# The last mixing steps of a graph layer: operands moved from SBUF to PSUM, and a list of steps scheduled anew

## The chip, the cores and the metric

The kernel runs on one core of one Trainium2 chip. The metric is the device time of one execution in microseconds; where several runs are shown, their median. Five engines work side by side, each through its own queue in order: TensorE (PE; its weight loads are PEld), VectorE (DVE), ScalarE (ACT), GpSimd (POOL) and SyncE (SP), which here only issues transfers. TensorE writes its results to the eight banks of PSUM; the other memory on the core is SBUF. [...]

## The reference

Four graph layers follow one another over x (8 batches, 2048 nodes, 64 features) and one adjacency matrix (2048 x 2048); each is `x = layernorm(x + layer(x, adj))`. The change lies in the end of layer 1, whose last lines and normalization are:

```
pair = jnp.stack([industry, g], axis=2)
coefs2 = jax.nn.softmax(attn_scores(pair), axis=-1)
out = jnp.einsum('bnk,bnkf->bnf', coefs2, pair)
...
def attn_scores(f):
    return jnp.tanh(f @ fcW + fcb) @ av
...
x = _layernorm(x + out, axis=-1)
```

`industry` is the adjacency applied to a projection of x, and `g` comes from attention over hyperedges. A softmax over two is a sigmoid of the difference of the two scores, and the kernel computes it so: with s = tanh(difference / 2), the mix is g + 0.5 (1 + s) (industry - g).

## The kernel before, in words

A tile is 128 nodes by 512 values (8 batches of 64 features), and there are 16 tiles. Layer 0 and the preparation of layer 1 take the first 660 us. Layer 1 then works on 16 tiles in a software pipeline: each tile has some forty small steps, and several tiles are under way at once. The order is written out by hand, as one long string of tokens at the end of `layer1` (L1183 to L1258): `3.m0` is step m0 of tile 3. `perform` calls the steps in this order, and `program_order` (L213) makes the queues of TensorE, VectorE, ScalarE and GpSimd keep it; SyncE's transfers may go ahead of it, as far as free buffers allow. Since each queue is in order, an instruction that waits holds everything behind it on its engine.

The steps of one tile j:

- `i` (L656), eight times: four matmuls of 128 x 512 each (L1918) into the bank `ind`, the adjacency product; `ind` (L668) is ScalarE's copy of it to SBUF. `mask` and `xr` and the start of `sx` are transfers from HBM.
- `sx`, `ST`, `gates`, `tau` (L866 to L905): small gate values. `gp`, `dp`, `red` are matmuls (L936, L954, L985), `m`, `z`, `e`, `g` VectorE's steps on 1024 or 512 values (L944, L947, L966, L988), `exp` and `t3` ScalarE's (L950, L960), `ch`, `w`, `a0`, `ga` GpSimd's (L925, L971, L978, L981). Together they make `g`, one SBUF row of 512 values.
- The mixer (L1001 to L1116): `dlt` (L1008) is industry - g; `xg` (L1018) is g + x on GpSimd, in the row `r`; `tr`, `sT`, `fc`, `th`, `sub` turn both inputs, multiply them with fcW and take the tanh; `df` (L693, in `by_columns`) multiplies by av and leaves the score differences in one PSUM bank; `rw` (L1055) is the tanh of the difference, `rt` (L168) turns it with two transposes into the other half of the same bank, so that each node has its eight shares there, in eight separate columns (`column_view`).
- Then the steps of the change: `sw` (L1065), ScalarE copies the eight shares to SBUF; `mult` (L1071), VectorE makes dlt = (share + 1) dlt; `r` (L1076), r = 0.5 dlt + r; `s` (L1082), the sum over 64 features; `centre` (L1086), r = r - s / 64. All of them read and write SBUF rows, apart from the copy's source.
- `sq`, `var`, `rstd`, `x2` (L1092 to L1106): squares on ScalarE, their sum on VectorE, the inverse root on GpSimd, eight scaled copies on ScalarE.

Layer 2's first steps stand in the tail of the same list: `f` (transposes), `xT`, `mm` (L1146), `hi`, `add`, `lo` (L1152 to L1160), and `A`, the first adjacency products.

PSUM is divided among pools in this part: one bank for the adjacency product, two for gathers (`g`), two single-bank buffers with the tag "m", which `dp`, `red`, the two turned rows and layer 2's `f` take in turns, one bank "sm" that `sx` and `df` take in turns, and two for `fc`. A step that needs a buffer waits until the last reader of what was in it is done. In the list before, 80 steps take an "m" buffer. The score bank "sm" is free again when ScalarE's copy `sw` has read it.

Of the kernel before, what the change touches and what calls it, by code (L numbers as in the profile page):

```python
# [9 lines left out]
F32 = mybir.dt.float32  # L10
# [3 lines left out]
ALU = mybir.AluOpType  # L14
# [49 lines left out]
def kernel(  # L64
# [547 lines left out]
    def layer1(  # L612
# [76 lines left out]
        def by_columns(dst, th):  # L689
            for half in range(2):  # L690
                for h in range(2):
                    k = 2 * half + h
                    nc.tensor.matmul(  # L693
                        dst[32 * k:32 * k + 32, 0:2 * P], av32,
                        th[:, h, half * 2 * P:(half + 1) * 2 * P],
                        start=True, stop=True, tile_position=(0, 32 * k),
                    )

        def column_view(src):
            return src[:, 2 * P:4 * P].rearrange(  # L700
                "p (l f h e) -> p l f h e", l=2, f=2, h=2
            )[:, :, :, :, 0]
# [6 lines left out]
        with tc.tile_pool(name="fa", bufs=2) as fa:  # L709
# [10 lines left out]
            with program_order():  # L720
# [69 lines left out]
                def capped():  # L790
                    c["ese"] = fa.tile([P, B], F32, tag="ese", name="ese", bufs=1)
                    nc.vector.tensor_scalar(
                        c["ese"].rearrange("p (f l h) -> p l f h", l=2, h=2),
                        column_view(c["sp"]), TOP, None, op0=ALU.min,
                    )
# [206 lines left out]
        def mixer(j):  # L1002
# [60 lines left out]
            def shares():  # L1063
                t["sw"] = small("sw", f"sw_{j}")
                nc.scalar.copy(  # L1065
                    t["sw"].rearrange("p (f l h) -> p l f h", l=2, h=2), column_view(t["df"])
                )

            def shared():
                dlt = b_view(t["dlt"])  # L1070
                nc.vector.scalar_tensor_tensor(  # L1071
                    dlt, bcast(t["sw"]), 1.0, dlt, op0=ALU.add, op1=ALU.mult
                )

            def mixed():
                nc.vector.scalar_tensor_tensor(  # L1076
                    t["r"], t["dlt"], 0.5, t["r"], op0=ALU.mult, op1=ALU.add
                )

            def summed():  # L1080
                t["s"] = small("s", f"s_{j}")
                nc.vector.tensor_reduce(t["s"], b_view(t["r"]), AX.X, ALU.add)  # L1082

            def centred():
                r = b_view(t["r"])
                nc.vector.scalar_tensor_tensor(  # L1086
                    r, bcast(t["s"]), -1.0 / C, r, op0=ALU.mult, op1=ALU.add
# [10 lines left out]
            def deviation():  # L1098
                nc.gpsimd.tensor_scalar(t["var"], t["var"], EPS, None, op0=ALU.add)
                t["rstd"] = small("rstd", f"rstd_{j}")  # L1100
                nc.gpsimd.tensor_tensor(t["rstd"], t["var"], mhalf, ALU.pow)

            def normed():
# [8 lines left out]
                rw=rows, rt=rows_turned, sw=shares, mult=shared, r=mixed, s=summed, centre=centred,  # L1112
# [67 lines left out]
        with program_order():  # L1180
            perform(
                (
                    "0.xr 1.xr c.rests 0.sx 0.dp 0.ST 0.gates 0.gp0 0.tau 1.sx 0.ch0 0.m0 0.gp1 1.ST "  # L1183
                    "1.dp 1.gates 0.m1 0.ch1 1.tau 2.sx 0.z0 1.i 1.ch0 0.t3 2.gates 1.i 0.exp0 0.z1 "
                    "1.i 2.tau 0.e0 0.exp1 1.gp0 1.ch1 2.ST 0.e1 1.ind 2.i 0.w0 1.t3 1.m0 1.gp1 2.i "
                    "1.z0 0.w1 2.i 0.a0 1.exp0 2.i 1.m1 0.ga 1.e0 0.red 3.sx 1.z1 2.ch0 2.gp0 3.ST "
                    "2.dp 0.g 1.exp1 2.m0 1.w0 0.tr0 2.i 0.sT0 1.e1 0.tr1 2.i 2.z0 0.xg 2.xr 0.sT1 "
                    "0.fc0 0.dlt 2.exp0 1.a0 3.gates 2.i 0.th0 1.w1 2.e0 2.i 3.tau 0.fc1 2.ind 2.ch1 "
                    "2.gp1 0.th1 3.i 2.m1 2.w0 2.t3 0.sub 1.red 4.sx 1.ga 2.z1 3.dp 4.ST 4.gates 2.a0 "
                    "3.i 2.exp1 1.g 0.df 4.tau 3.ch0 2.e1 1.tr0 0.rw 3.i 1.sT0 1.dlt 0.rt 3.gp0 2.w1 "  # L1190
                    "0.sw 0.mult 1.fc0 3.m0 1.tr1 1.th0 3.i 1.xg 3.xr 0.r 1.sT1 3.z0 3.i 2.ga 1.fc1 "
                    "0.s 3.exp0 3.ch1 0.centre 3.i 1.th1 3.e0 2.red 3.t3 1.sub 4.ch0 5.sx 3.gp1 2.g "
                    "5.ST 3.i 0.sq 3.m1 3.w0 2.dlt 2.tr0 3.i 5.mask 3.z1 2.sT0 2.fc0 3.ind 2.xg 4.xr "
                    "5.gates 3.exp1 4.i 0.var 3.a0 5.tau 1.df 3.e1 2.tr1 1.rw 0.rstd 4.i 2.th0 4.gp0 "
                    "2.sT1 1.rt 4.dp 4.m0 1.sw 3.w1 0.x2 4.i 1.mult 4.z0 2.fc1 4.ch1 4.i 1.r 4.exp0 "
                    "3.ga 1.s 3.red 2.th1 4.e0 6.sx 4.t3 3.g 4.i 5.ch0 1.centre 4.gp1 2.sub 6.ST 4.i "
                    "1.sq 3.xg 5.xr 4.m1 3.tr0 3.tr1 1.var 3.sT0 4.i 4.w0 3.sT1 4.z1 3.fc0 6.gates "
                    "4.exp1 5.dp 1.rstd 3.dlt 6.tau 4.e1 2.df 4.i 6.mask 3.th0 4.a0 5.gp0 4.ind 3.fc1 "
                    "5.m0 4.w1 2.rw 1.x2 2.rt 5.i 5.z0 5.i 5.ch1 2.sw 5.exp0 2.mult 4.red 4.ga 2.r "
                    "5.t3 7.sx 5.e0 5.i 4.g 7.ST 6.ch0 3.th1 5.gp1 2.s 4.tr0 5.m1 4.tr1 4.sT0 5.i "  # L1200
                    "4.dlt 5.w0 4.sT1 5.z1 6.dp 3.sub 5.exp1 5.i 4.xg 6.xr 2.centre 4.fc0 5.e1 5.a0 "
                    "2.sq 5.i 2.var 5.w1 6.gp0 7.gates 5.i 6.m0 7.tau 3.df 6.ch1 5.i 7.mask 3.rw 6.z0 "
                    "4.th0 3.rt 5.ga 5.red 5.ind 4.fc1 6.exp0 2.rstd 5.g 5.dlt 6.i 3.sw 6.t3 6.e0 "
                    "5.tr0 6.i 3.mult 5.sT0 7.ch0 6.gp1 4.th1 3.r 8.sx 6.m1 2.x2 6.i 3.s 6.w0 6.z1 "
                    "5.tr1 6.i 8.ST 4.sub 5.sT1 5.xg 7.xr 7.dp 6.exp1 3.centre 5.fc0 6.a0 6.e1 3.sq "
                    "6.i 3.var 6.w1 7.gp0 8.gates 6.i 7.m0 8.tau 4.df 3.rstd 6.i 4.rw 7.z0 5.th0 4.rt "
                    "6.i 8.mask 7.exp0 6.ga 6.red 6.ind 7.e0 7.ch1 5.fc1 4.sw 3.x2 4.mult 8.ch0 9.sx "
                    "6.g 7.gp1 9.gates 7.t3 7.i 6.xg 8.xr 7.m1 6.tr0 6.dlt 7.i 6.sT0 7.z1 7.w0 9.ST "
                    "5.th1 6.tr1 8.dp 4.r 7.exp1 5.sub 7.i 7.a0 9.tau 7.e1 6.sT1 5.df 6.fc0 5.rw 4.s "
                    "7.w1 8.gp0 4.centre 6.th0 5.rt 7.i 8.m0 5.sw 4.sq 8.ch1 6.fc1 5.mult 8.z0 7.ga "  # L1210
                    "7.i 8.t3 7.red 4.var 8.exp0 5.r 4.rstd 7.i 7.g 6.th1 10.sx 8.e0 7.i 10.ST 4.x2 "
                    "6.sub 9.ch0 7.tr0 7.i 9.mask 5.s 10.gates 8.gp1 7.sT0 8.w0 9.dp 7.ind 8.m1 "
                    "5.centre 10.tau 6.df 8.z1 5.sq 8.i 7.xg 9.xr 6.rw 7.fc0 7.dlt 8.exp1 8.a0 5.var "
                    "8.i 7.th0 8.e1 5.rstd 7.tr1 8.i 7.sT1 9.gp0 8.w1 8.i 5.x2 9.m0 6.rt 8.i 9.z0 "
                    "6.sw 9.ch1 7.fc1 6.mult 9.exp0 8.ga 8.i 6.r 9.t3 8.red 9.e0 8.i 8.g 10.ch0 7.th1 "
                    "6.s 9.gp1 8.tr0 9.m1 8.i 10.mask 8.sT0 6.centre 9.w0 10.dp 9.z1 8.ind 6.sq 9.i "
                    "7.sub 9.exp1 8.xg 10.xr 11.sx 6.var 8.fc0 9.a0 9.e1 11.ST 8.tr1 11.gates 6.rstd "
                    "9.i 8.sT1 8.dlt 11.tau 7.df 10.gp0 8.th0 9.w1 9.i 10.m0 7.rw 8.fc1 6.x2 10.z0 "
                    "7.rt 10.ch1 9.i 10.exp0 9.ga 9.red 9.i 10.t3 10.e0 9.i 9.g 11.ch0 8.th1 10.gp1 "
                    "9.i 7.sw 10.m1 10.w0 7.mult 12.sx 10.z1 9.i 11.mask 12.ST 9.tr0 7.r 9.ind 9.xg "  # L1220
                    "11.xr 11.dp 12.gates 9.sT0 10.exp1 9.dlt 9.tr1 10.a0 10.i 8.sub 9.sT1 12.tau "
                    "10.i 10.e1 8.df 7.s 10.w1 10.i 8.rw 7.centre 8.rt 9.fc0 7.sq 8.sw 7.var 11.ch1 "
                    "10.i 9.th0 8.mult 7.rstd 11.gp0 8.r 11.t3 10.i 11.m0 10.red 10.ga 7.x2 8.s 10.i "
                    "11.z0 13.sx 10.g 11.exp0 10.i 8.centre 10.xg 12.xr 13.gates 10.tr0 13.ST 8.sq "
                    "10.i 12.mask 11.e0 10.sT0 12.dp 10.ind 8.var 12.ch0 11.gp1 10.dlt 11.i 11.m1 "
                    "10.tr1 13.tau 11.z1 11.w0 11.i 9.fc1 11.exp1 8.rstd 11.i 9.th1 11.e1 11.i 10.sT1 "
                    "9.sub 11.a0 8.x2 12.gp0 11.i 12.m0 11.w1 9.df 10.fc0 12.z0 9.rw 12.ch1 9.rt "
                    "10.th0 11.i 11.ga 11.red 12.exp0 11.i 12.t3 12.e0 10.fc1 11.g 12.w0 9.sw 12.gp1 "
                    "9.mult 10.th1 11.i 13.mask 12.m1 11.tr0 10.sub 11.ind 13.ch0 14.sx 11.sT0 12.i "
                    "12.z1 14.ST 11.fc0 12.a0 11.dlt 12.exp1 14.gates 12.i 11.xg 13.xr 12.e1 14.tau "  # L1230
                    "10.df 12.i 9.r 11.th0 12.w1 9.s 13.gp0 10.rw 12.i 13.m0 10.rt 13.ch1 12.i 10.sw "
# [1433 lines left out]
```

## Time and profile before

| what | value |
|---|---|
| time before, median of 3 runs | 1230.51 us (1228.17 to 1231.52) |
| the profiled execution | 1229.4 us, its span 1227.7 us |
| busy over the span: PE / DVE / ACT / POOL | 97% / 74% / 32% / 42% |
| granted TensorE clock over the span | 0.995 |
| VectorE's busy time in slices 23 to 30 of 40 | about nine tenths |
| DMA | 157.10 MB, mean 128 GB/s |

The profile is one execution, recorded by the hardware. "Busy" is the time with an instruction in work; matmuls are pipelined and their ends are modelled, so a busy TensorE is not a full one. A row of a group names the line, the engine, the operation, output <- inputs, the shapes and the count; then busy us and mean ns of one; then how long the engine idled just before these instructions, and what ended that. A timeline row gives start and duration in us first. A row of waits gives the engine and line that waited, what it waited for, and then us in total, times, and the longest.

### The profile page before, as it was taken

To read this page: it belongs to the slowest core of one execution; us is meant where nothing else is said; L and a number is where in the kernel's file an instruction comes from. 1 tells how busy PE (TensorE), PEld (TensorE's weight loads), DVE (VectorE), ACT (ScalarE), POOL (GpSimd) and SP (SyncE) were. 2 spreads that over 40 slices of the span, in tenths; PEclk is the share of its full clock that TensorE was granted. 3 is DMA by queue.
4 is the path that set the end of the run, shared out by engine and by line. 5 is a ranking of instruction groups with operands and counts; after the bars stand their busy time and mean duration, and the time that the engine had idled before them with its cause. 6 is when DMAs were issued, how large, how long until landed. Compare 5 with 4: busy or idle time off the path is not lost.

```text
span 1227.7 us, 19772 instructions
## 1 busy us (share of the span) xinstructions
PE 1187.7 (97%) x7470; PEld 942.0 (77%) x7470; DVE 911.2 (74%) x1671; ACT 388.8 (32%) x1019; POOL 512.4 (42%) x429
## 2 busy tenths in 40 slices
PE   9999899999999999999999999999999999999996
PEld 7777788888888888888886655555557788888885
DVE  4555678888888888888876899988996766665454
ACT  3100102222222222222223667676676411111111
POOL 2000472555555555555511788888881700000000
PEclk9999999999999999999998999999999999999998
DMA  8977943333333333332384113122320333334541
GB/s 282 251 230 222 189 131 104 109 105 113 109 103 107 114 115 114 106 99 99 106 309 147 43 61 110 62 103 104 95 69 2 138 132 109 118 123 163 180 172 71
DMA packets 101848, 157.10 MB, mean 128 GB/s; under 512 B 13041, under 2 KB 64369, under 8 KB 96113
## 3 DMA queue, kind: packets, MB, share of 16 engines
q1 hardware_dynamic: 96944, 151.38, 38.4%
q10 hardware_dynamic: 4368, 4.33, 1.0%
q8 instruction: 61, 1.00, 0.4%
q0 software_dynamic: 432, 0.05, 0.1%
q14 instruction: 43, 0.34, 0.1%
HBM read 117.97 MB, written 37.76 MB: 127 GB/s over the span
## 4 chain that ended last, share of the span: by engine, by line
PE 73%; DVE 13%; DMA 4%; issue 3%; ACT 3%; POOL 2%; SPq 0%; DVEq 0%; ACTq 0%; POOLq 0%
PE pp L1457 26%; PE a L1918 19%; PE y2p L1414 9%; PE y1p L569 5%; PE ind L1918 3%; DMA xraw<-in_xn 2%; DVE d L947 2%; DVE ez L966 1%; DVE gp L944 1%; PE u L1146 1%; DMA adj<-in_at 1%; PE yp L2017 1%; PE try L168 1%; DVE r L1086 1%; PE hp L1582 1%
## 5 line engine op out<-in xcount | busy, mean ns | idle before, releaser
L1468 DVE SCALAR_TENSOR_TENSOR r<-pp,emb_sb,r 128x256 f32<-128x256 f32 x512 | 247.4, 483 | 78.1 <-PE pp L1457 63.9
L1457 PE MATMUL pp<-w_sb,xT 64*128 64x256 f32 x1024 | 155.4, 380 | 0.6 <-DVE r L1468 0.6
L1457 PE MATMUL pp<-w_sb,y2T 64*128 64x256 f32 x1024 | 153.5, 376 | 2.4 <-DVE y2T L1430 2.4
L1457 PE MATMUL pp<-w_sb,y1T 64*128 64x256 f32 x1024 | 153.3, 376 | 0.0
L1326 POOL TENSOR_TENSOR ms<-msk,srow 128x1024 f32<-128x1024 f32 x30 | 76.5, 2552 | 93.8 <-DVE msk L449 93.8
L1457 PEld LDWEIGHTS pp<-w_sb,y2T 64*128 64x128 f32 x1024 | 99.3, 187 | 14.0 <-DVE y2T L1430 2.8
L1457 PEld LDWEIGHTS pp<-w_sb,y1T 64*128 64x128 f32 x1024 | 99.4, 187 | 11.2
L1457 PEld LDWEIGHTS pp<-w_sb,xT 64*128 64x128 f32 x1024 | 95.1, 187 | 12.9 <-issue 2.8
L569 PE MATMUL y1p<-x_hi,m 128*128 128x512 f32 x256 | 103.0, 402 | 1.1 <-DVE y_lo L584 1.1
L569 PE MATMUL y1p<-x_lo,m 128*128 128x512 f32 x256 | 100.5, 393 | 0.0
L1918 PE MATMUL a<-v_hi,mj_l 128*128 128x512 f32 x256 | 100.1, 392 | 0.0
L1918 PE MATMUL a<-v_lo,mj_l 128*128 128x512 f32 x256 | 100.0, 391 | 0.0
L1918 PE MATMUL a<-y_lo,mj_l 128*128 128x512 f32 x240 | 95.1, 396 | 0.0
L1918 PE MATMUL a<-y_hi,mj_l 128*128 128x512 f32 x240 | 94.9, 396 | 0.0
L1414 PE MATMUL y2p<-y_hi,msk 128*128 128x512 f32 x240 | 94.7, 395 | 0.0
L1414 PE MATMUL y2p<-y_lo,msk 128*128 128x512 f32 x240 | 93.5, 390 | 0.0
L1918 PE MATMUL ind<-y_hi,mj_l 128*128 128x512 f32 x208 | 91.2, 438 | 0.1
L1918 PE MATMUL ind<-y_lo,mj_l 128*128 128x512 f32 x208 | 81.9, 394 | 0.0
L971 POOL TENSOR_TENSOR ez<-ez,coef 128x1024 f32<-128x1024 f32 x32 | 65.2, 2039 | 12.8 <-DVE ez L966 12.7
L1366 DVE SCALAR_TENSOR_TENSOR ms<-ms,adj 128x1024 f32<-128x1024 f32 x30 | 67.3, 2242 | 0.0
L1649 POOL TENSOR_TENSOR hs<-h,es 128x512 f32<-128x512 f32 x15 | 15.6, 1042 | 116.1 <-ACT hgr L1621 116.1
L925 POOL TENSOR_TENSOR d<-h,sig 128x1024 f32<-128x1024 f32 (+1 forms) x32 | 50.1, 1569 | 32.6 <-ACT sig L903 18.3
(335 smaller groups left out, 2448.8 us busy)
## 6 DMA issues: line engine op xcount, KB each, us to landing
mj_l<-mask SPq DMA_DIRECT2D x44, 1024.0 KB, 5.0
adj<-in_at SPq DMA_DIRECT2D x64, 256.0 KB, 3.8
mask<-msk SPq DMA_DIRECT2D x32, 512.0 KB, 4.5
raw<-in_at SPq DMA_DIRECT2D x31, 512.0 KB, 5.8
oh<-oh SPq DMA_DIRECT2D x32, 128.0 KB, 4.1
xT<-in_xt SPq DMA_DIRECT2D x16, 256.0 KB, 3.2
xs<-in_xn SPq DMA_DIRECT2D x16, 256.0 KB, 2.7
kept<-x SPq DMA_DIRECT2D x16, 256.0 KB, 3.4
```

What stands on the lines that cost most here:

```text
L168: nc.tensor.matmul(dst, src, ident, start=True, stop=True, is_transpose=True)
L569: nc.tensor.matmul(accs[q][jj], r_(m[:, t, jj * P:(jj + 1) * P]), r_(part[:, mt, :]), start=i + h + t == 0 and part is x_hi, stop=i == 3 a ...
L925: nc.gpsimd.tensor_tensor(d[:, 0:n].rearrange("p u (b c) -> p u b c", b=B), b_view(h_sb[:, j, :]).unsqueeze(1).to_broadcast([P, n, B, C]), ...
L947: nc.vector.tensor_tensor(ds[i], ds[i], gps[i], ALU.add)
L971: nc.gpsimd.tensor_tensor(by_b(ezs[i]), by_b(ezs[i]), per_b(t["coef"], 2 * i, 2), ALU.mult)
L1326: nc.gpsimd.tensor_tensor(ms, m, srow[j].unsqueeze(1).to_broadcast([P, 8, P]), ALU.mult)
L1366: nc.vector.scalar_tensor_tensor(ms, ms, 1.0, raws[j][h], op0=ALU.mult, op1=ALU.not_equal, accum_out=bad[:, 2 * j + h:2 * j + h + 1],)
L1414: nc.tensor.matmul(acc, r_(msk[j, mt // 8][:, mt % 8, :]), r_(part[:, mt, :]), start=mt == 0 and part is y_hi, stop=mt == NT - 1 and part ...
L1457: nc.tensor.matmul(pp[:, h, pl, :], terms[j][name][rs, 2 * bq + pl], w_sb[rs, k, dq * 4 * C:(dq + 1) * 4 * C], start=k == 0, stop=k == K - 1,)
L1468: nc.vector.scalar_tensor_tensor(rb, ppv[:, :, dd, :], emb_sb[:, j, d:d + 1], rb, op0=ALU.mult, op1=ALU.add)
L1649: nc.gpsimd.tensor_tensor(b_view(hs), b_view(h_sb[:, j, :]), bcast(es[:, j, :]), ALU.mult)
L1918: nc.tensor.matmul(acc, r_(a[:, mt, :]), r_(part[:, mt, :]), start=mt == 0 and part is hi, stop=mt == NT - 1 and part is lo,)
```

## The change

The copy `sw` goes. `mult` reads the shares where the transposes left them, in the score bank, and writes its product to a new tile `mx` in one of the two "m" buffers; `r` adds the row r to `mx` in place; `s` sums `mx`; `centre` reads `mx` and writes the SBUF row r, which `sq` and `x2` read as before. So the score bank is now free after VectorE's `mult`, and an "m" buffer is taken from `mult` to `centre`: 96 steps of the new list take one. For `mult` to read the eight columns in their natural order, `by_columns` takes its moving operand in another order of 128-wide blocks and `column_view` becomes a plain stride; the step `ese` for the edges (L792) uses the same view. The small tile `rstd` is requested a line earlier, in the same step.

The list of steps is a new one (1007 tokens, before 1023: the 16 `sw` are gone). Its steps for one tile keep their dependences, but their places between those of other tiles differ throughout; in the start `gp0` stands ahead of `dp`, for instance. From `dp` to `t3`, the steps between which the product dp lives in its buffer, there are 19.8 tokens on average over tiles 1 to 13, before 31.5.

```diff
--- before.py
+++ after.py
@@ -692,14 +692,12 @@
                     k = 2 * half + h
                     nc.tensor.matmul(
                         dst[32 * k:32 * k + 32, 0:2 * P], av32,
-                        th[:, h, half * 2 * P:(half + 1) * 2 * P],
+                        th[:, h].rearrange("p (l f e) -> p f l e", f=2, e=P)[:, half],
                         start=True, stop=True, tile_position=(0, 32 * k),
                     )
 
         def column_view(src):
-            return src[:, 2 * P:4 * P].rearrange(
-                "p (l f h e) -> p l f h e", l=2, f=2, h=2
-            )[:, :, :, :, 0]
+            return src[:, 2 * P:4 * P].rearrange("p (b e) -> p b e", b=B)[:, :, 0]
 
         head = (
             "1.mask 2.mask 3.mask 4.mask c.agg 0.i c.hexp c.he 0.ind c.trhe c.agg1 c.heT "
@@ -790,8 +788,7 @@
                 def capped():
                     c["ese"] = fa.tile([P, B], F32, tag="ese", name="ese", bufs=1)
                     nc.vector.tensor_scalar(
-                        c["ese"].rearrange("p (f l h) -> p l f h", l=2, h=2),
-                        column_view(c["sp"]), TOP, None, op0=ALU.min,
+                        c["ese"], column_view(c["sp"]), TOP, None, op0=ALU.min,
                     )
 
                 def exp_scores():
@@ -1060,31 +1057,26 @@
                         t["df"][:, (2 + l) * P:(3 + l) * P], t["rows"][:, l * P:(l + 1) * P]
                     )
 
-            def shares():
-                t["sw"] = small("sw", f"sw_{j}")
-                nc.scalar.copy(
-                    t["sw"].rearrange("p (f l h) -> p l f h", l=2, h=2), column_view(t["df"])
-                )
-
             def shared():
-                dlt = b_view(t["dlt"])
+                t["mx"] = ps_m.tile([P, BC], F32, tag="m", name=f"mx_{j}")
                 nc.vector.scalar_tensor_tensor(
-                    dlt, bcast(t["sw"]), 1.0, dlt, op0=ALU.add, op1=ALU.mult
+                    b_view(t["mx"]), bcast(column_view(t["df"])), 1.0, b_view(t["dlt"]),
+                    op0=ALU.add, op1=ALU.mult,
                 )
 
             def mixed():
                 nc.vector.scalar_tensor_tensor(
-                    t["r"], t["dlt"], 0.5, t["r"], op0=ALU.mult, op1=ALU.add
+                    t["mx"], t["mx"], 0.5, t["r"], op0=ALU.mult, op1=ALU.add
                 )
 
             def summed():
                 t["s"] = small("s", f"s_{j}")
-                nc.vector.tensor_reduce(t["s"], b_view(t["r"]), AX.X, ALU.add)
+                nc.vector.tensor_reduce(t["s"], b_view(t["mx"]), AX.X, ALU.add)
 
             def centred():
-                r = b_view(t["r"])
                 nc.vector.scalar_tensor_tensor(
-                    r, bcast(t["s"]), -1.0 / C, r, op0=ALU.mult, op1=ALU.add
+                    b_view(t["r"]), bcast(t["s"]), -1.0 / C, b_view(t["mx"]),
+                    op0=ALU.mult, op1=ALU.add,
                 )
 
             def squared():
@@ -1096,8 +1088,8 @@
                 nc.vector.tensor_reduce(t["var"], b_view(t["sq"]), AX.X, ALU.add)
 
             def deviation():
+                t["rstd"] = small("rstd", f"rstd_{j}")
                 nc.gpsimd.tensor_scalar(t["var"], t["var"], EPS, None, op0=ALU.add)
-                t["rstd"] = small("rstd", f"rstd_{j}")
                 nc.gpsimd.tensor_tensor(t["rstd"], t["var"], mhalf, ALU.pow)
 
             def normed():
@@ -1109,7 +1101,7 @@
 
             steps = dict(
                 dlt=difference, xr=fetch, xg=residual, th0=tanh0, th1=tanh1, sub=lessened, df=scores,
-                rw=rows, rt=rows_turned, sw=shares, mult=shared, r=mixed, s=summed, centre=centred,
+                rw=rows, rt=rows_turned, mult=shared, r=mixed, s=summed, centre=centred,
                 sq=squared, var=variance, rstd=deviation, x2=normed,
             )
             for i in range(2):
@@ -1180,81 +1172,80 @@
         with program_order():
             perform(
                 (
-                    "0.xr 1.xr c.rests 0.sx 0.dp 0.ST 0.gates 0.gp0 0.tau 1.sx 0.ch0 0.m0 0.gp1 1.ST "
...
-                    "0.sw 0.mult 1.fc0 3.m0 1.tr1 1.th0 3.i 1.xg 3.xr 0.r 1.sT1 3.z0 3.i 2.ga 1.fc1 "
...
-                    "14.centre 8.xT 15.sub 1.A 7.hi 10.f 9.xT 2.A 7.add 14.sq 15.df 7.lo 8.mm/f 15.rw "
...
+                    "0.xr 1.xr c.rests 0.sx 0.gp0 0.ST 0.gates 0.gp1 0.tau 1.sx 0.ch0 0.m0 1.i 1.ST "
...
+                    "1.dlt 1.fc0 1.sT1 2.a0 2.e1 3.i 1.th0 0.mult 2.w1 3.gp0 0.r 1.fc1 3.m0 3.ch1 3.i "
...
+                    "5.hi 1.A 5.add 6.xT 15.fc1 5.lo 14.s 7.f 15.th1 14.centre 6.mm/g 7.xT 15.sub 8.f "
...
```

## The prediction

> **What bounds the kernel now.** I read the rows of the 40 slices first, then windows over the stretch that the change touches, then VectorE's groups, its waits and the timeline of single instructions. The mixing steps of layer 1 (L1008 to L1106) run from 699 to 961 us, so I cut there:
>
> ```profile
> core 0: us, PE busy (x) PEld busy (x) DVE busy (x) ACT busy (x) POOL busy (x), PEclk, DMA share, GB/s
> ...
> 685.00:925.00 240.00, 224.94 (x1050) 139.10 (x1048) 219.15 (x288) 164.13 (x428) 201.43 (x135) 1.00 0.25 82
> 925.00:965.00 40.00, 39.81 (x390) 30.37 (x391) 27.95 (x45) 28.77 (x67) 12.21 (x12) 1.00 0.14 53
> ```
>
> VectorE is busy for 219.15 of 240 us (91%), GpSimd for 84%, ScalarE for 68%. TensorE's 225 is too high, since matmul records overlap. I took the distance from each matmul's start to the next and, as undisturbed, the 15th percentile of the distances between the same two kinds (0.228 us within L1918). The sum is 203 us of work and 37 us of waits: 85%. So this stretch is VectorE's, with TensorE and GpSimd close behind. From 925 to 965 VectorE is at 70%: there layer 2's projections follow one another at 1.68 us each.
>
> VectorE's waits in the stretch are few:
>
> ```profile
> DVE ez L966 <- ACT gp L950: 7.1, 5, 2.1
> DVE gp L944 <- PE gp L936: 7.0, 7, 1.4
> DVE var L1096 <- ACT sq L1092: 1.5, 2, 0.8
> ```
>
> No wait of more than 0.2 us in all stands before L1071, L1076, L1082 or L1086. These four are not late; they are long:
>
> ```profile
> L1086 DVE SCALAR_TENSOR_TENSOR r<-s,r 128x512 f32<-128x512 f32 x14 | 20.2, 1445 | 0.2
> ...
> L1071 DVE SCALAR_TENSOR_TENSOR dlt<-sw,dlt 128x512 f32<-128x512 f32 x14 | 17.2, 1227 | 0.2
> L1076 DVE SCALAR_TENSOR_TENSOR r<-dlt,r 128x512 f32<-128x512 f32 x14 | 16.8, 1203 | 0.2
> ...
> L988 DVE TENSOR_TENSOR g<-g,red 128x512 f32<-128x512 f32 x16 | 10.8, 677 | 0.8 <-POOL var L1099 0.8
> L1082 DVE TENSOR_REDUCE s<-r 128x8 f32<-128x512 f32 x14 | 9.5, 676 | 0.2
> ```
>
> All write 512 values or reduce them. L988, with one operand in PSUM, takes 677 ns; its 16 lie between 670 and 689. L1071 lies between 677 and 2442. The timeline shows why; VectorE, then GpSimd:
>
> ```profile
> 828.48 2.44 DVE L1071 SCALAR_TENSOR_TENSOR dlt<-sw,dlt 128x512 f32<-128x512 f32 x1
> ```
>
> ```profile
> 828.47 1.90 POOL L971 TENSOR_TENSOR ez<-ez,coef 128x1024 f32<-128x1024 f32 x1
> ```
>
> GpSimd began 0.01 us earlier and ended at 830.37; VectorE's ended 0.55 us after that, and its record contains the 1.9 us it stood still. Where GpSimd rests (after 940 us) L1071, L1076 and L1086 all take 0.68 to 0.69. So in this trace a VectorE instruction that reads two SBUF operands is held by a GpSimd instruction, and one with an operand in PSUM is not.
>
> **The change part by part.** *shared, mixed, centred.* Each now has one SBUF operand (dlt, r, s) and one in PSUM (df, then mx twice). In the stretch: 20.2 + 17.2 + 16.8 = 54.2 us for 42 instructions; as undisturbed ones 42 x 0.687 = 28.9 us, a saving of 25.3 us. I take 687 ns from L944's 512-wide form, which like mixed reads PSUM and SBUF and writes PSUM. The tail's instances are undisturbed already and save nothing. No row shows a scalar_tensor_tensor whose first operand is eight PSUM columns, each repeated 64 times. From below it costs 677 (L988), from above today's mean of 1158 over all 16, which is 16 x 0.47 = 7.5 us dearer. I take 687, since repeated SBUF operands (L944's rest) cost nothing extra.
>
> *summed* reads PSUM in place of SBUF. The row says 676 against L988's 677, so nothing. [...] The rows show no such difference (677 with PSUM, 676 without, undisturbed SBUF pairs 680 to 690), and I take the rows. [...]
>
> *shares.* 16 ScalarE copies of 172 ns go (2.8 us). ScalarE is at 68%, so nothing by itself; the step from the turned rows to the product loses one hop. In its place VectorE waits for TensorE's turn (L168), and behind it in VectorE's queue stand L944, L947 and L966, for which ScalarE's exponentials and GpSimd wait. In the list the product follows its turn by 4.1 steps on average (tiles 1 to 13), before by 9.7. With some 860 steps in 245 us a step is 0.28 us, so 1.1 us of cover are left. Bounds: -0.2 us a tile (the copy's time) to +0.5 us a tile (half of that cover missing), -3 to +8 us in all; I take 0, as L168 directly before L1065 made ScalarE wait three times, 2.2 us together.
>
> *The score bank* ("sm", one buffer) is now freed by VectorE's product, not by the copy. TensorE's next sx or df is queued behind it. From df to the release the list has 16.4 steps on average, before 17.7: nothing.
>
> *The strided slice* in by_columns reads two runs of 128 in place of one of 256 and issues as many matmuls. Eight take 0.64 us (L693); I take no change, at worst twice (16 x 0.64 = 10 us), at best nothing.
>
> *GpSimd.* What held VectorE also held GpSimd: L971 takes 2039 ns against 1.90 us undisturbed, L1018 1516, L981 1414 and L978 1435 against 1.28. That is 4.4 + 3.5 + 2.1 + 2.3 = 12 us that may go; 201 - 12 = 189. L1008 still reads two SBUF rows and keeps part of it, and its 990 ns.
>
> *The list.* What moves on SP's queue are the transfers of oh, xr and the masks. From the step that frees a buffer to its first use there are 54 steps or more in both lists after the first three sx, 15 us; the transfers land in 2.5 to 5.7 us. Nothing. The start is shuffled (gp0 before dp); I count no gain.
>
> *The bank of mx.* mx takes one of the two "m" banks from product to centring, where dp, red and the turned shares lived alone. In the stretch dp holds a bank for 10 us a tile (L954 to the last L960), red about 1.5, the two turned shares 1.3 each; L1071's start to L1086's end is 7.4 us. Per tile of 16 us and two banks (32 us): 14 before, 21.5 after. The new list shortens dp to t3 from 31.5 to 19.8 steps, so I expect about 18. If red or a turned share meets two taken banks, TensorE stands still, with all its matmuls behind. In the tail one bank is left for layer 2's transposes while mx lives (24 steps for tiles 14 and 15, three allocations within). A transpose with its copy needs 0.35 + 0.59 us and two hand-overs, under the 1.68 us of a projection; I put 1 us for it (0 to 3).
>
> *The sum.* After it VectorE needs 219.15 - 25.3 = 193.9 us, GpSimd about 190, TensorE 203. What is late next is TensorE. The leading engine of today reaches 91%; with three of nearly equal load I take 90%: 203 / 0.90 = 225.6, so 14.4 us less, and 1 us back in the tail: 13.4. The profiled execution took 1229.4 (span 1227.7 and 1.7 around it), so 1216.0; the median lies 1.1 above it: 1217.
>
> **The rivals.** *TensorE closes up (18%).* Ten microseconds of TensorE's waits are for L966, which frees the gather's bank, so they are VectorE's lateness. If most such waits go, it reaches 93%: 203 / 0.93 = 218.3, -22: 1209. Against it: fc, df and the turns also wait for ScalarE.
>
> *The freed time turns into other waits (12%).* TensorE's waits are a hundred small ones of 0.2 to 1.5 us, set by the order of the list. If the product's wait costs its upper bound (8 us) and the repeated PSUM operand 4, 2 us remain: 1228. That the change does not do what it says, because GpSimd also holds instructions with one SBUF operand, ends here too. L988's narrow spread speaks against it.
>
> *Slower: the two "m" banks run out (8%).* If dp keeps its 10 us and mx its 7.4 of a 16 us tile, both are taken for 0.62 x 0.46 = 29% of the time. Three allocations a tile that each meet this once in 3.4 and wait 2 us cost 1.7 us a tile, 28 us in all, against 14 gained; with the list's shorter dp I put 20: 1236. It decides from 0.9 us of bank wait a tile on.
>
> **How the numbers follow.** My case has 62%: 1217, between 88% and 92% (1222 to 1212). The range reaches from 1207 to 1228 and leaves out the far end of the first rival, half of the second and the third, under 2 in 10. About 0.3% (3.7 us) can be told from no change, so faster means under 1226.8. My case and the first rival are faster, 80%, and a little of the second: 82%. Most of the second is the same: 10%. The third is slower: 8%.
>
> **What would show it.** In the profile after: the product, mixing and centring lines at 0.68 to 0.70 us with no instance above 0.8; L1082's successor at 0.68 [...]; L971's mean near 1.95; the stretch at 224 to 228 us with VectorE at 86% and TensorE's waits for L966 fewer. It is wrong if the product's mean is near 1.2, if VectorE shows waits for L168 of over 5 us, or if TensorE's turned shares or red wait for the centring line by more than 5 us.

## The result, and the profile after

The changed kernel takes 1214.91 us (median of 4 runs, 1211.86 to 1216.58); the kernel before, in its runs of the same comparison, 1231.01 (1228.17 to 1235.98). The ratio is 0.9867, its 95% interval 0.9829 to 0.9905. The prediction said 1217, within 1207 to 1228. The span of the profiled execution fell from 1227.7 to 1212.4 us.

First the four lines of the change, as groups of VectorE between 670 and 950 us of the changed kernel: busy us and mean ns, then the idle time just before them and what ended it. Above them stands `dlt` (L1005), which still reads two SBUF rows.

```profile
L1005 DVE SCALAR_TENSOR_TENSOR dlt<-ind,g 128x512 f32<-128x512 f32 x16 | 15.9, 996 | 1.8 <-ACT ind L668 1.8
L1068 DVE SCALAR_TENSOR_TENSOR mx<-mx,r 128x512 f32<-128x512 f32 x16 | 11.2, 698 | 0.5
L1062 DVE SCALAR_TENSOR_TENSOR mx<-df,dlt 128x512 f32<-128x512 f32 x16 | 11.1, 694 | 3.9 <-PE df L168 2.7 <-ACT th L1038 1.0
...
L1077 DVE SCALAR_TENSOR_TENSOR r<-s,mx 128x512 f32<-128x512 f32 x16 | 10.9, 683 | 0.2
L1074 DVE TENSOR_REDUCE s<-mx 128x8 f32<-128x512 f32 x16 | 10.9, 682 | 0.1
```

The product, the mixing and the centring went from 1227, 1203 and 1445 ns in the stretch (1158, 1139 and 1350 over all 16) to 694, 698 and 683, and no instance of theirs is above 0.70 us. The sum went from 676 to 682. `dlt`, which the change leaves alone, took 971 ns over all 16 before and takes 996 now. At the right end of L1062's row stand 3.9 us of waiting that L1071 did not have before.

GpSimd has not got out of the way. Of the 48 instances of product, mixing and centring, 34 start while GpSimd has one of its wide instructions in work, and they take 0.68 to 0.70 us like the other 14. In the kernel before 30 of the 48 start so and take 1.53 us on average; the other 18 take 0.68 to 0.69. One mixing step of the changed kernel, VectorE and then GpSimd:

```profile
808.74 0.70 DVE L1068 SCALAR_TENSOR_TENSOR mx<-mx,r 128x512 f32<-128x512 f32 x1
```

```profile
808.67 1.90 POOL L968 TENSOR_TENSOR ez<-ez,coef 128x1024 f32<-128x1024 f32 x1
```

Next the windows, with busy us of each engine and in brackets the instructions:

```profile
core 0: us, PE busy (x) PEld busy (x) DVE busy (x) ACT busy (x) POOL busy (x), PEclk, DMA share, GB/s
...
685.00:910.00 225.00, 224.43 (x1069) 142.77 (x1069) 195.41 (x293) 164.59 (x423) 190.28 (x136) 1.00 0.26 88
910.00:950.00 40.00, 39.62 (x388) 29.95 (x387) 29.43 (x45) 29.02 (x65) 10.34 (x11) 1.00 0.13 50
```

The first row covers the work that took 685 to 925 before. VectorE is busy for 195.41 of 225 us, 87% in place of 91%; GpSimd for 190 us in place of 201. TensorE's own column is again too high: a matmul of the adjacency product (L1909) has a record of 0.40 us, and the next one starts 0.23 us after it (medians). By the distances of its starts, worked out as in the prediction, it has about 198 us of work in the 220 us from 685 to 905, 90% in place of 85%. This is an estimate. If the two lines alone tell the pairs of matmuls apart, the same distances give 188 us before (78%) and 183 after (83%); the rise of five points is the same.

For the gain itself I take two marks on VectorE: the first gather sum of the stretch (`g<-g,red`) and layer 2's first `x<-u,x`. Before they stand at 695.0 and 931.1 us, 236.1 apart; after at 696.8 and 915.1, 218.3 apart. The stretch gave 17.8 us. The tail, from there to layer 2's first `r<-a,s,x`, took 35.6 us before and 36.1 after. The other way, 1.8 us were lost ahead of the first mark, where the granted clock was low for longer (shown at the end).

Last, what still makes VectorE and TensorE wait from 685 to 910:

```profile
DVE gp L941 <- PE gp L933: 6.7, 9, 1.5
DVE d L944 <- ACT d L957: 5.6, 3, 2.8
DVE gate L888 <- PE sx L168: 5.0, 3, 3.4
DVE mx L1062 <- PE df L168: 2.7, 4, 1.1
```

```profile
PE trm L168 <- DVE g L985: 0.5, 2, 0.3
```

The second block is the only row of TensorE's matmuls. Its waits for VectorE's steps (df for L1047 4.0 us, gp for L966 3.7, and others) are gone. Its weight loads waited for the centring line twice, 1.2 us together; this is all of the price of mx's bank that shows there.

### The profile page after: what moved, and what is told of

Read it like the earlier page. It is cut to its first block, busy times and chain, and to the rows that moved or that the text cites. A ratio compares the mean times of both kernels' runs of the same rounds, so it can differ in the third digit from the quotient of the medians.

```text
span 1212.4 us, 19761 instructions
## 1 busy us (share of the span) xinstructions
PE 1185.2 (98%) x7470; PEld 945.0 (78%) x7470; DVE 889.8 (73%) x1671; ACT 386.7 (32%) x1003; POOL 500.5 (41%) x429
## 5 line engine op out<-in xcount | busy, mean ns | idle before, releaser
L1909 PE MATMUL a<-v_hi,mj_l 128*128 128x512 f32 x256 | 100.1, 392 | 0.0
L1909 PE MATMUL a<-v_lo,mj_l 128*128 128x512 f32 x256 | 100.0, 391 | 0.0
L1909 PE MATMUL a<-y_lo,mj_l 128*128 128x512 f32 x240 | 95.1, 396 | 0.0
L1909 PE MATMUL a<-y_hi,mj_l 128*128 128x512 f32 x240 | 94.9, 395 | 0.0
L1909 PE MATMUL ind<-y_hi,mj_l 128*128 128x512 f32 x208 | 90.5, 435 | 0.0
L1909 PE MATMUL ind<-y_lo,mj_l 128*128 128x512 f32 x208 | 81.9, 394 | 0.0
L968 POOL TENSOR_TENSOR ez<-ez,coef 128x1024 f32<-128x1024 f32 x32 | 61.6, 1927 | 11.1 <-DVE ez L963 11.0
L1909 PEld LDWEIGHTS ind<-y_hi,mj_l 128*128 128x128 f32 x208 | 39.3, 189 | 26.7 <-issue 17.3
```

Source lines behind the costliest of these rows:

```text
L968: nc.gpsimd.tensor_tensor(by_b(ezs[i]), by_b(ezs[i]), per_b(t["coef"], 2 * i, 2), ALU.mult)
L1909: nc.tensor.matmul(acc, r_(a[:, mt, :]), r_(part[:, mt, :]), start=mt == 0 and part is hi, stop=mt == NT - 1 and part is lo,)
```

## The experiments

The change has three parts: the operands in PSUM, the bank that holds them, and the list. The first runs take them apart; the next group asks which engine sets the time; the last asks what an order alone does.

**1. The new steps in the old list.** The old list can't be kept as it is: counted over its tokens, mx from product to centring would make a third "m" buffer necessary at 46 places. So mixing, sum and centring stand directly behind the product for tiles 0, 1, 2, 4, 7, 10, 14 and 15, and tile 4's product after tile 6's gather sum. Tile 0's part of it:

```diff
-"... 0.sw 0.mult 1.fc0 3.m0 1.tr1 1.th0 3.i 1.xg 3.xr 0.r 1.sT1 3.z0 ..."
+"... 0.mult 0.r 0.s 0.centre 1.fc0 3.m0 1.tr1 1.th0 3.i 1.xg 3.xr 1.sT1 3.z0 ..."
```

> The new steps (product, mixing and sum in a PSUM bank, no copy of the shares) under the order of the kernel before. Where the old order would have three holders of the two m buffers, the mixing, sum and centring of that tile stand directly behind its product (tiles 0, 1, 2, 4, 7, 10, 14, 15), and tile 4's product stands later. My theory (VectorE loses 25 us of standing still, and the new order turns this into time): the three lines fall to 0.69 us here too, VectorE's busy time in the stretch falls by about 25 us, but the order is not fitted to it, so about 9 us of the 16 come: 1221 against 1230. Rival 1 (the list does it, the bank is incidental): within 3 us of before. Rival 2 (the bank does it alone): 15 to 17 us less, as the changed kernel.

Measured: 1229.8 us, ratio 1.0019 (0.9999 to 1.0039): no gain. Yet the four lines took 693, 698, 688 and 683 ns, and VectorE was busy for 199.60 us from 685 to 925, 19.6 less than before. Most of what it saved it waited for:

```profile
DVE gp L941 <- PE gp L933: 14.9, 14, 2.2
...
DVE ez L963 <- ACT gp L947: 10.0, 7, 2.1
...
DVE g L985 <- PE red L982: 4.2, 4, 1.7
```

These are waits of 7.0 and 7.1 us before, and the third was not there. By the two marks the stretch took 230.5 us in the trace, 5.6 less than before. But 3.4 us were lost ahead of the first mark, where the clock was 0.75 over 660 to 685 us (0.86 before), and 2.6 in the tail. For the waits two explanations are left: the bank makes TensorE late, or the pulled order does. Runs 11 and 12 bear on this.

**2. The old steps in the new list.** The copy `sw` stands directly ahead of the product of its tile (tile 0's shown), and all rows are in SBUF.

```diff
-"... 3.i 1.th0 0.mult 2.w1 3.gp0 0.r ..."
+"... 3.i 1.th0 0.sw 0.mult 2.w1 3.gp0 0.r ..."
```

> The new order with the steps of before (SBUF rows; ScalarE's copy of the shares stands directly ahead of the product). My theory: VectorE still stands still for 25 us behind GpSimd and stays the bound at 91% of the stretch, so -3 to +6 us against before, and the three lines have means of 1.1 to 1.4 us. Rival 1 (the list does it): 12 us or more less. Rival 2 (the bank alone): the same as before within 3 us.

Measured: 1249.09 us, ratio 1.0173 (1.0128 to 1.0218). With the old steps the new list costs 21 us. The three lines are long again (1229, 1229 and 1101 ns), and VectorE waits for the copy, which the old list put up to 7 steps ahead of its product:

```profile
DVE dlt L1071 <- ACT sw L1065: 13.2, 9, 3.4
```

```profile
685.00:925.00 240.00, 218.04 (x983) 135.16 (x983) 205.99 (x273) 151.57 (x403) 188.25 (x127) 0.96 0.24 79
```

The granted clock (0.96) is below full in this window, where before and after have 1.00. This loss joins long lines, the wait for the copy and a lower clock; how much each has of it stays open.

**3 and 9. The shares alone,** in the new list (3) and in the old one (9): the product reads PSUM and writes its SBUF row; mixing, sum and centring are those of before; no bank is held.

```diff
-                t["mx"] = ps_m.tile([P, BC], F32, tag="m", name=f"mx_{j}")
+                t["mx"] = t["dlt"]
...
```

> The changed kernel, but only the shares are read from PSUM: the product goes to its SBUF row, mixing and centring read two SBUF operands again, and no m buffer is taken. My theory: only the product's line falls to 0.69 us, mixing and centring keep 1.1 to 1.4 us, so a third of VectorE's saving (about 8 of 25 us) is left and some 5 us of time: 1225 against 1230. Rival (what counts is the copy that is gone and the hand-over that it cost): nearly all of the gain is here, 13 us or more.

> The old order, and of the new steps only the shares read from PSUM (no copy, product into its SBUF row, no m buffer held). VectorE loses about 7 us of standing still. Under the first reading (m buffers ate it): 4 to 7 us less than before. Under the second (the old order): within 3 us of before. Under the new order the same steps gave 4 us.

Measured: 1221.35 us in the new list, ratio 0.9969 (0.9950 to 0.9987), and 1229.84 in the old one, ratio 0.9969 (0.9939 to 0.9999); they ran on different chips, so the ratios are to be compared. The product fell to 683 ns in the new list, the other two stayed long:

```profile
L1068 DVE SCALAR_TENSOR_TENSOR r<-dlt,r 128x512 f32<-128x512 f32 x16 | 20.5, 1284 | 0.5
L1077 DVE SCALAR_TENSOR_TENSOR r<-s,r 128x512 f32<-128x512 f32 x16 | 18.7, 1171 | 0.2
L1062 DVE SCALAR_TENSOR_TENSOR dlt<-df,dlt 128x512 f32<-128x512 f32 x16 | 10.9, 683 | 3.5 <-PE df L168 2.6 <-ACT th L1038 0.9
```

Here a single operand in PSUM freed the one instruction that has it (683 ns) and no other line of the mixing (1284 and 1171 ns). Against the kernel before, both runs come to 3.8 us less. In run 9 this is the part alone. In run 3 it is the part and the new list together: against the old steps in that list (run 2) it is 2.0%, in which the waits for the copy and the clock are contained. From run 3 to the whole change the ratio goes from 0.9969 to 0.9867, 1.0% or some 12 us. That is what mixing and centring get from the row in PSUM, in this list.

**4 and 5. Less TensorE.** Of the four matmuls of each step `i` (L656) two are left, those of `i_hi`, for before (4) and for after (5). The product lacks its low part. This takes away 240 matmuls, and at the 0.228 us between two of them 55 us of TensorE's work, nearly all of it in the stretch.

```diff
-                    times_mask(acc_of[j], mask_of[j], i_hi, i_lo, mt)
+                    nc.tensor.matmul(
+                        acc_of[j], r_(mask_of[j][:, mt, :]), r_(i_hi[:, mt, :]),
+                        start=mt == 0, stop=mt == NT - 1,
+                    )
```

> The kernel before, with work of TensorE left out: the low half of the split operand in the industry products of tiles 1 to 15 (240 of 480 matmuls, 55 us of TensorE at 0.228 us each), so that industry is computed with fewer bits. If VectorE bounds the stretch of before, as the prediction had it: at most 5 us less (1222 against 1227), TensorE's share falls and VectorE stays at 91%. If the order of the old list makes TensorE the late one, as the run of the new steps under the old order suggests: 12 us or more less.

> The changed kernel with the same 240 matmuls left out. If TensorE bounds the stretch now: VectorE's 195 us at 91 to 95% become the bound, 205 to 214 in place of 225 us, so 11 to 20 us less than the changed kernel, 0.97 to 0.98 of before. If VectorE still does: no more than 5 us less than the changed kernel, 0.982 to 0.987. [...]

Measured: 1.0011 (0.9993 to 1.0028) for before, no time gained. The stretch took 235.4 us in place of 236.1, with VectorE busy for 217.72 us from 685 to 925, 91% as before. One reservation: the clock was 0.983 on average over these runs and 0.994 over those of before, and a lower clock goes with a longer time here (last section), so some gain may be hidden. For after 0.9793 (0.9760 to 0.9826) against 0.9867, some 9 us (3 to 15 by the two intervals); the stretch took 212.4 us in place of 218.3. TensorE matters after the change, but far less than its work: 55 us taken away, 6 to 9 gained.

**6 and 7. More VectorE.** The sum over 64 features is made three times, for before (6) and after (7, where the sum reads `mx`): 32 further instructions of 0.68 us, 21.7 us in all.

```diff
+                nc.vector.tensor_reduce(t["s"], b_view(t["r"]), AX.X, ALU.add)
+                nc.vector.tensor_reduce(t["s"], b_view(t["r"]), AX.X, ALU.add)
```

> The kernel before, with the sum over features computed three times in place of once (32 more reductions of 0.60 us start to start, 19 us of VectorE in all, 17 of them in the stretch; no result changes). If VectorE bounds it: 15 to 19 us more, 1243 to 1246. If the order does, with VectorE having slack: under 10 us more.

> The changed kernel with the sum computed three times, as in the run before this one. If TensorE bounds the stretch and VectorE has slack (86% busy): 4 to 10 us more than the changed kernel. If VectorE still bounds it: 15 to 19 us more, so that the gain is gone.

Measured: 1.0202 (1.0165 to 1.0239) for before, 25 us (20 to 29), all that was added. For after 1.0034 (1.0002 to 1.0065) against 0.9867, some 20 us (14 to 27). So VectorE's time still comes through nearly whole after the change, though VectorE is busy for only 87%.

**8. Before without the centring.** VectorE's L1086 is left out (20.2 us in the stretch), so the rows are not centred; no bank is held.

```diff
             def centred():
-                r = b_view(t["r"])
-                nc.vector.scalar_tensor_tensor(
-                    r, bcast(t["s"]), -1.0 / C, r, op0=ALU.mult, op1=ALU.add
-                )
+                pass
```

> The kernel before with the centring left out (the mean is not subtracted, so the normalization is another). VectorE loses 20.2 us in the stretch, as much as the new steps saved under the old order (19.6), and no m buffer is held. If VectorE's time bounds the old order and the held m buffers ate the gain of the new steps under the old order: 14 us or more less than before. If the old order itself lets nothing come of a freed VectorE (TensorE's and ScalarE's steps follow at their places): within 4 us of before.

Measured: 1221.21 us, ratio 0.9894 (0.9858 to 0.9931), 13 us, between the two expectations; the stretch took 226.7 us, 9.4 less. In the old list VectorE's time brings about half to two thirds of itself when it is taken away, and costs all of itself when it is added.

**10. A busier TensorE ahead of the stretch.** In the changed kernel nine matmuls without use, in two new steps, fill a pause of TensorE at 663 to 666 us. The granted clock of its profile drops some 10 us later.

```diff
-"... 0.ind c.trhe c.agg1 c.heT c.fche ..."
+"... 0.ind c.fill6 c.trhe c.agg1 c.heT c.fill3 c.fche ..."
```

> The changed kernel with nine more matmuls (128 x 512, into a bank that is overwritten) where TensorE stands still between 663 and 666 us, ahead of the turn of the edges' rows and of their fully connected step. In the profile of the changed kernel the granted clock was one half from 675 to 686 us, after this pause. If the pause causes it: the clock stays at 1 there, and 3 to 5 us less than the changed kernel (0.983 of before). If not: the same clock, and 0 to 1 us more.

Measured: 1211.7 us, ratio 0.9832 (0.9787 to 0.9877), not to be told from the 0.9867 of the change. The clock was still at half speed from 680 to 685 us; over 675 to 680 it was 0.86, in the changed kernel 0.51. So filling this pause does not remove the spell. With one trace of each, it is not shown whether it shortened it.

**11. The pulled order alone.** All steps as before, in the order of run 1, with `sw` where it was.

```diff
-"... 0.sw 0.mult 1.fc0 3.m0 1.tr1 1.th0 3.i 1.xg 3.xr 0.r 1.sT1 3.z0 ..."
+"... 0.sw 0.mult 0.r 0.s 0.centre 1.fc0 3.m0 1.tr1 1.th0 3.i 1.xg 3.xr 1.sT1 3.z0 ..."
```

> The kernel before, all its steps as they were (copy of the shares, all rows in SBUF), with only the order of the run with the new steps in the old list: the mixing, the sum and the centring directly behind the product for tiles 0, 1, 2, 4, 7, 10, 14 and 15, and tile 4's product after tile 6's gather sum. It asks whether those moved steps ate the 19.6 us of VectorE that the new steps saved there. If the moved steps did: 5 to 13 us slower than before (1.004 to 1.010). If the held bank did: no difference, 0.998 to 1.002.

Measured: 1249.99 us, ratio 1.0182 (1.0140 to 1.0225). To set mixing, sum and centring directly behind the product for eight of 16 tiles costs 22 us, more than either theory had put down. VectorE waits for the gather (it was 7.0 us before), while the granted clock is 0.95:

```profile
DVE gp L944 <- PE gp L936: 16.6, 12, 3.1
DVE ez L966 <- ACT gp L950: 9.7, 7, 2.1
DVE g L988 <- PE red L985: 4.2, 3, 2.6
```

```profile
685.00:925.00 240.00, 218.30 (x991) 137.31 (x990) 203.85 (x273) 153.43 (x400) 190.03 (x127) 0.95 0.24 79
```

The three waits are nearly those of run 1 (14.9, 10.0 and 4.2 us), and here no bank is held. So they come with the order. The time follows the clock as well: the six runs reach from 1237.76 us at a mean clock of 0.992 to 1255.23 at 0.983.

Run 1 minus this run is the worth of the new steps in this order: 1.0019 against 1.0182, some 20 us. They did gain in run 1; the order, with the lower clock that came with it, had lost as much.

**12. The same, with a bank held.** In the order of run 11 one "m" buffer is taken from the copy to the centring, and the wide rows stay in SBUF.

```diff
+                t["mx"] = ps_m.tile([P, BC], F32, tag="m", name=f"mx_{j}")
+                nc.scalar.copy(t["mx"][:, 0:B], t["df"][:, 2 * P:2 * P + B])
...
-                nc.vector.tensor_reduce(t["s"], b_view(t["r"]), AX.X, ALU.add)
+                nc.vector.tensor_reduce(t["mx"][:, 0:B], b_view(t["r"]), AX.X, ALU.add)
...
+                nc.vector.tensor_copy(t["s"], t["mx"][:, 0:B])
```

> The same kernel and order as the previous run, and one of the two m buffers is held in addition from the product to the centring, as the changed kernel holds it, without the gain of operands in PSUM for the wide instructions: ScalarE makes a second copy of eight columns into the held bank (172 ns a tile, beside other work), the sum goes into eight columns of it, and VectorE copies these to SBUF ahead of the centring [...]. If the held bank eats the gain under the old order: 8 to 16 us over the previous run. If it doesn't: 1 to 3 us over it.

Measured: 1251.75 us, ratio 1.0194 (1.0151 to 1.0237), 1.5 us over run 11 and not to be told from it; by the intervals a cost of up to some 9 us is not excluded. The bank is waited for, on TensorE:

```profile
PE trm L168 <- DVE s L1087: 6.7, 3, 3.7
PE red L985 <- DVE s L1087: 3.8, 2, 3.6
...
PE dp L954 <- DVE s L1087: 1.9, 1, 1.9
```

L1087 is the copy ahead of the centring, the last reader of the held bank; it took 0.15 to 0.17 us in six tiles. Twelve microseconds of waiting for it changed the stretch by 0.4 us (252.7 in run 11, 253.1 here). Perhaps other waits stand ahead of these in this order; that was not tried. It is not shown what the bank would cost in an order that is bound by nothing else.

Side by side, as ratios to the kernel before:

| steps | order of before | pulled order | new list |
|---|---|---|---|
| as before | 1 | 1.018 | 1.017 |
| shares alone | 0.997 | not run | 0.997 |
| all of the change | needs a third buffer | 1.002 | 0.987 |

Within a column the new steps gain: 1.6% in the pulled order, 3.0% in the new list. Within a row the order matters too: 1.7 to 1.8% lost from the first column to the others with the old steps, 1.5% gained from the pulled order to the new list with the new ones. Part of the upper row's loss goes with a lower clock, and in its last field with the copy's place. No run with the new steps alone or the new list alone came near the 1.3%: the change is a pair.

## Why the prediction was right, and where it was not

*The bound before.* It held. VectorE's share of 91% meant what it seemed to: runs 4, 6 and 8 give nothing for 55 us of TensorE (with the reservation of run 4), 25 us for 21.7 more of VectorE and 13 for 20.2 less.

*The lines.* The sum took 687 ns each; they came to 694, 698 and 683. The stalls are gone in every list that gives the line an operand in PSUM: means of 683 to 698 ns for the three lines in run 1, 683 for the product in run 3, and 0.68 us for it in run 9 (its four instances from 900 us on). They stay in every list that does not: 1229, 1229 and 1101 ns in run 2, 1173, 1426 and 1093 in run 11, mixing and centring at 1284 and 1171 in run 3 and at up to 2.37 and 2.08 us from 900 us on in run 9; and in `dlt` (996 ns). That 34 of the 48 ran beside GpSimd without a stall is what the prediction had read from L988's narrow spread (670 to 689 ns). The undecided bound, eight PSUM columns repeated 64 times as first operand, was settled at 694 against an upper end of 1158. Reading PSUM made the lines hardly longer: the sum takes 682 ns from PSUM against 676 from SBUF, 6 ns more, and the mixing and centring are within 18 ns of their undisturbed SBUF form (680 to 690).

*GpSimd.* Twelve microseconds were said to be free; eleven went. L968's row shows a third of it, with 2039 ns before:

```profile
L968 POOL TENSOR_TENSOR ez<-ez,coef 128x1024 f32<-128x1024 f32 x32 | 61.6, 1927 | 11.1 <-DVE ez L963 11.0
```

*The product's wait* was put at nothing between -3 and +8; it is 2.7 us for L168, and 1.0 for the tanh before it. *The tail's* 1 us is 0.6.

*What is late next.* This step was half right. The prediction set TensorE's 203 us over an assumed 90% and got 225.6 us, 14.4 less than 240; the stretch gave 17.8. But if TensorE alone were the bound, run 5 had to gain the 11 to 20 us that its expectation names, and gained 6 to 9; and run 7 had to lose 4 to 10, and lost some 20. After the change VectorE still sets most of the time, and TensorE has a part in it. The assumed 90% came near the estimate of 83 to 90% after, but the argument behind it named the wrong engine as the only one. GpSimd, busy for 84% before and 85% after, was varied in no run, so its part stays open.

*The rivals.* The second, freed time turning into other waits, is what run 1 did for the most part: of 19.6 us of VectorE freed, the stretch gained 5.6 and the whole kernel nothing. In the changed kernel, with another list, the stretch gained 17.8 of about 24. The third put a bound on the bank: 20 us, if dp keeps its buffer and mx lives 7.4 us. In the trace after, mx lives 4.9 us on average (2.9 to 8.0). The prediction had counted the three lines at their old lengths, 1.6 us a tile more, and the new list sets the centring closer behind the product (15.2 tokens on average over tiles 1 to 13, before 22.5). The waits for the bank were 1.2 us. Whether the old order would have made the bank dear stays open, as run 12 can only be read in an order that was already late.

*What the prediction did not ask.* It used the new list for the cover of single waits and for the bank, but gave the order as a whole no term, as if it were neutral. Runs 2 and 11 show that an order, with the clock that comes with it, can move the time by 1.7 to 1.8% here, more than the change itself. In the pulled order the same new steps ended at 1.0019. So it is in part luck that the number came out: the 90% stood in for an order whose effect was not worked out.

## What to carry to other kernels

When VectorE instructions have long and widely spread durations, look at what GpSimd does at the same moment before you look at the instruction: here an operand in PSUM took such lines from about 1300 to 690 ns, each one only for itself. Freed time on an engine became gain here only as far as the order let it: 13 of 20 us in run 8, 5.6 of 19.6 us in the stretch of run 1. Test the steps and the order apart before you credit either. A busy share of 87% did not acquit VectorE here: add a known amount of work to an engine and see whether the time follows.

## What was not expected of the hardware

In these profiles the granted TensorE clock drops to 0.5 for spells of 3 to 10 us, at places that differ between them (665.1 to 671.9 us before, 675.1 to 685.4 after). Around the start of layer 1's pipeline, the kernel before and then the changed one, with the clock behind the busy columns:

```profile
660.00:685.00 25.00, 22.66 (x107) 15.31 (x107) 15.43 (x54) 8.81 (x29) 5.06 (x6) 0.86 0.40 119
```

```profile
660.00:685.00 25.00, 22.42 (x96) 15.99 (x96) 14.89 (x49) 6.58 (x23) 5.10 (x6) 0.80 0.39 115
```

In runs 2, 4, 6, 11 and 12 such spells fall inside the stretch, and its mean is 0.95 to 0.96. There they follow pauses of TensorE. In run 11 it waited 4.35 us for VectorE from 789.9 us on, and the clock was down from 792 to 799:

```profile
794.25 1.08 PE L693 MATMUL df<-th,av 128*32 128x256 f32 x8 [4.35 <-DVE th L1047]
```

```profile
790.00:800.00 10.00, 5.75 (x22) 2.68 (x24) 6.82 (x14) 5.89 (x14) 5.28 (x4) 0.66 0.00 1
```

Between 690 and 945 us the profiles of all 14 kernels have 26 spells. Each begins within a pause of TensorE of 1.2 us or more (by the modelled ends of its matmuls), or at most 3.5 us behind it. Of the pauses of 2 us and more 19 of 28 were followed so, of the shorter ones 7 of 40. The stretches of before, after and run 10 have no pause above 1.4 us and no spell. The spell ahead of the stretch, at 675 to 685 us after the change, has no such pause just before it; its cause stays open.

What does a lower clock go with? Among the 42 runs of before that stand beside runs 1 to 3, the time goes from 1223.5 us at a mean clock of 0.997 to 1240.3 at 0.988, by a straight line 1.3 us for each 0.001. By this estimate the lower clock of runs 2, 4 and 11 (0.983 to 0.986, against 0.994 to 0.996 of before beside them) goes with 12 to 14 us in each. That would be more than half of what runs 2 and 11 lose, and a gain of that size could be hidden in run 4. It is a correlation: a list with more waits may be slow for the waits and slow for the clock, and the two were not tried apart. The gain of the change itself is no such effect: its four runs have 0.990 to 0.996, no higher than before.
